# Where the transposes of the quantized activations stand among the self-attention's tiles

## The chip, the core and the metric

The kernel runs on one core of a Trainium2 chip. The core has a matrix engine (TensorE, PE in the profile; its weight loads are PEld), a vector engine (VectorE, DVE), a scalar engine (ScalarE, ACT), GpSimd (POOL) and SyncE (SP), which here only issues DMAs. Each engine works through its own queue in order; semaphores make one wait for another. PE writes into PSUM, eight banks of 128 partitions by 512 floats; DVE and ACT read PSUM, POOL does not. The metric is the device time in microseconds of one execution, here the median of three runs.

## The reference

The layer takes `x` (16 x 64 x 1024, so 1024 rows) and a context (16 x 1024 x 1024) and computes, in float32:

```
x = x + cross_attention(layernorm(x), ctx)         # 32 heads, 8 key/value heads, 32 wide
x = x + self_attention(layernorm(x))               # the same heads, rotary positions, 64 keys each
x = x + ffn(layernorm(x))

ffn(x):
    beta = mean(|x|) per row
    xq   = clip(round(x * sqrt7 / (beta + eps)), -8, 7) * beta      # 4-bit activations
    gate = xq @ ternary(w_gate).T * scale;  up = xq @ ternary(w_up).T * scale    # 1024 -> 2752
    inter = up * relu(gate)^2
    out  = int8(inter) @ ternary(w_down).T * scale                  # 2752 -> 1024
```

`ternary(w)` rounds `w / mean|w|` to -1, 0 or 1. The values of `xq` without their scale are small integers, so the feed-forward matmuls are done on bf16 activations against fp8 weights.

## The kernel before

The 1024 rows are eight tiles of 128 (two batches each). The kernel first does the cross-attention for all batches (up to about 1305 us), then the output projection and the second layer norm, and then, from about 1486 us, the part that the change touches. All order is written by hand: the program's text is the order on every engine.

**The loop over tiles (lines 1250 to 1304).** Iteration `t` (0 to 8) works on two tiles of the self-attention at once: `two` is tile t, whose scores are made, and `last` is tile t-1, which is finished. Its parts, in order:
- `transpose3(t - 2)`: eight PE transposes (L941) of the 4-bit activations of tile t-2 from `xq3` into one PSUM bank, and one ACT copy (L942) from there into `xqT[t - 2]`, the left operand of the gate/up matmuls.
- `two.by_key()`: 32 small matmuls (L781) into `w`, which fills four PSUM banks, and two ACT copies (L791) to SBUF.
- `last.subtract()` (DVE L830): the scores less their maxima, which come back by DMA.
- `last.exponentials()` (ACT L833), `last.values()` (PE L841 and L852 into the same `w`, then ACT copies L860 and L863), `last.finish()` (PE transposes L873 and L876, DVE L878 and L883, then the residual sum on POOL, L889).
- `two.maxima(0)`, `two.maxima(1)` (DVE L800, L801) and `two.row()` (DVE L813, L817; then SP sends the maxima to DRAM, L821, and fetches them back spread over partitions, L825).
- `quantize(t - 1)` in four pieces on DVE with a little POOL: `statistics` (L187 and after; needs L889), `magnitude` (L179, L921), `scaled` (L924 to L927), `rounded` (L930, L932; writes the single `xq3` buffer that the transposes read).

**Fillers.** Between these parts `fill()` takes the next piece of other PE work from a list. Up to t=3 these are pieces of the second half's key, value and query projection (24 pieces; a query chunk is two pieces and ends in `rotary`: ACT L719, DVE L720 and L721, POOL L722 and L723). From t=4 on they are 32 gate/up steps `(n, tt)`: column chunk n of 344 columns for row tile tt of 0 to 3. A step is 8 gate matmuls and 8 up matmuls (L959), a Relu on ACT (L967), a multiply on DVE (L968) and one on POOL (L971). After the last row tile of a chunk, `fetch(n + 3)` issues two DMAs on SP (L949) for weights of a later chunk. The iterations t=0 to 3 hold six fillers, t=4 nine (two ahead of `by_key`), t=5 to 7 seven, t=8 what is left. Only four pieces are left for t=3.

**PSUM banks.** `w` has four banks. The other four are m0, m1, t0 and t1. `four_tile` goes round them (m1, t0, t1, m0), and the even gate/up steps take t1 for the gate product and m0 for up, the odd steps m1 and t0. `transpose3` takes t0 or t1 through `t_tile`, which flips a bit at every allocation of a t bank, whoever makes it. A bank can be written again when its last reader is done: Relu for a gate product, DVE's multiply for an up product.

**The last loop (lines 1308 to 1334).** 32 more steps, chunks 0 to 7 for row tiles 4 to 7; the first nine are for tiles 4 to 6 and the tenth is the first on tile 7. Steps 0 and 1 use two banks (`m_tile`), from step 2 on the four banks of `w` are used. Beside given steps stand the quantization and the transposes of tile 7, the DMAs of the down weights (`fetch_down`), and from step 9 on the 8-bit quantization and down projection. After step 9 PE works on almost without a gap.

Of the kernel before, what the change touches and what calls it, by code (L numbers as in the profile page):

```python
# [25 lines left out]
NT = B * NQ // P  # L26
# [23 lines left out]
def kernel(  # L50
# [33 lines left out]
    def t_tile(shape, dtype, name, n=None):  # L84

        turns["t"] ^= 1
        n = turns["t"] if n is None else n
        return ps_t.tile(shape, dtype, tag=f"t{n}", name=name)

    def m_tile(name):  # L90
        turns["m"] ^= 1
        return ps_m.tile([P, 512], F32, tag=f"m{turns['m']}", name=name)

    def four_tile(name):

        turns["four"] = (turns["four"] + 1) % 4
        if turns["four"] < 2:
            return ps_m.tile([P, 512], F32, tag=f"m{turns['four']}", name=name)
        return t_tile([P, 512], F32, name, turns["four"] - 2)
# [10 lines left out]
    def place(kb, shape, dtype=F32):  # L110

        first, n = round(kb * 256), math.prod(shape) * mybir.dt.size(dtype)
        a = arena[:, first : first + (n + 3) // 4]
        if dtype != F32:
            a = a.bitcast(dtype)
        a = a[:, : math.prod(shape)]
        if len(shape) > 1:
            names = [f"a{i}" for i in range(len(shape))]
            sizes = dict(zip(names[1:], shape[1:]))
            a = a.rearrange(f"p ({' '.join(names)}) -> p {' '.join(names)}", **sizes)  # L120
        return a
# [790 lines left out]
    def quantize(t):  # L912

        xn = place(xn3_at, [DIM])
        statistics, normalize = layernorm(xn, xs[t], f"n3_{t}")
        b = beta[:, t : t + 1]
        rb = small.tile([P, 1], F32, tag="rb", name=f"rb_{t}")

        def magnitude():
            normalize()  # L920
            nc.vector.tensor_reduce(b, xn, AX.X, ALU.add, apply_absolute_value=True)  # L921

        def scaled():
            nc.vector.tensor_scalar_mul(b, b, 1.0 / DIM)  # L924
            nc.vector.tensor_scalar_add(rb, b, EPS)
            nc.vector.reciprocal(rb, rb)
            nc.vector.tensor_scalar(xn, xn, SQRT7, rb, ALU.mult, ALU.mult)  # L927

        def rounded():
            nc.vector.tensor_scalar(xn, xn, -8.0, 7.0, ALU.max, ALU.min)  # L930
            xq3[t] = place(xq_at, [DIM], BF)
            nc.vector.tensor_scalar(xq3[t], xn, MAGIC, MAGIC, ALU.add, ALU.subtract)  # L932
            nc.gpsimd.tensor_tensor(cgate[:, t : t + 1], b, wscale[:, 0:1], ALU.mult)
            nc.gpsimd.tensor_tensor(cup[:, t : t + 1], b, wscale[:, 1:2], ALU.mult)

        return [statistics, magnitude, scaled, rounded]

    def transpose3(t):
        tp = t_tile([P, KC, P], BF, f"xqp_{t}")
        for k in range(KC):  # L940
            nc.tensor.transpose(tp[:, k, :], xq3[t][:, bass.ts(k, P)], ident_b)  # L941
        nc.scalar.copy(xqT[t], tp)  # L942

    def fetch(n):

        wbs[n] = []
        for i in range(2):
            q = wb_ring.next([KC, CW], F8)
            nc.sync.dma_start(q.rearrange("p k o -> p (k o)"), ternary[i][n % NCH])  # L949
            wbs[n].append(q)  # L950

    def gate_up(n, t, banks):

        c = n % NCH
        relu, prod = relu_ring.next([CW]), prod_ring.next([CW])
        for i in range(2):
            ps = banks(i)
            for k in range(KC):
                nc.tensor.matmul(  # L959
                    ps[:, :CW],  # L960
                    lhsT=xqT[t][:, k, :],
                    rhs=wbs[n][i][:, k, :],
                    start=(k == 0),
                    stop=(k == KC - 1),
                )
            if i == 0:
                nc.scalar.activation(relu, ps[:, :CW], AF.Relu, scale=cgate[:, t : t + 1])  # L967
        nc.vector.scalar_tensor_tensor(  # L968
            prod, ps[:, :CW], cup[:, t : t + 1], relu, ALU.mult, ALU.mult
        )  # L970
        nc.gpsimd.tensor_tensor(inter[t][:, bass.ts(c, CW)], prod, relu, ALU.mult)  # L971
# [26 lines left out]
    def fetch_down():  # L998
        wd_rows = ternary_d.rearrange("c p f -> (c p f)").rearrange("(i h) -> i h", h=DIM)
        nc.gpsimd.memset(wds[NIC - 1][LAST:], 0.0)  # L1000
        for c0, c1 in ((0, 16), (16, NIC - 1)):
            nc.sync.dma_start(
                place(112 if c0 == 0 else 22, [c1 - c0, DIM], F8),
                wd_rows[c0 * P : c1 * P].rearrange("(c p) h -> p c h", p=P),
            )
        nc.sync.dma_start(wds[NIC - 1][:LAST], wd_rows[(NIC - 1) * P :])
# [43 lines left out]
    def fill(n=1):  # L1050
        for _ in range(n):
            if fillers:
                fillers.pop(0)()

    with tc.manual_schedule():
# [36 lines left out]
        tiles = [(kT, v)]  # L1092
        for n in range(2 * B):

            b = n // 2
            if n % 2 == 0:
# [8 lines left out]
                elif b + 1 < B:  # L1105
                    kT, v, steps = project_fast(b + 1)
# [14 lines left out]
            for i in range(4):  # L1121
# [25 lines left out]
                t = n // 4 - 1  # L1147
# [101 lines left out]
        two, last = None, None  # L1249
        for t in range(NT + 1):  # L1250
            two, last = (Tile2(t, w) if t < NT else None), two
            late = t >= NT // 2
            if t == NT // 2 - 2:
                for n in range(2):
                    fetch(n)
            if t == NT // 2:
                fill(len(fillers))
                fetch(2)
                steps = [(n, tt) for n in range(NCH) for tt in range(NT // 2)]

                steps[:12] = [s for s in steps[:12] if s[1] < 3] + [(n, 3) for n in range(3)]

                def beside(n, tt):
                    gate_up(n, tt, lambda i: four_tile(f"gu_{n}_{tt}_{i}"))
                    if tt == NT // 2 - 1:
                        fetch(n + 3)

                fillers += [lambda s=s: beside(*s) for s in steps]
            if t > 1:
                transpose3(t - 2)  # L1270
            if t == NT // 2:
                fill(2)
            pieces = quantize(t - 1) if last and two else []

            def piece():
                if pieces:
                    pieces.pop(0)()

            if two:
                two.by_key()  # L1280
            if last:
                last.subtract()
            fill()
            if last:
                last.exponentials()
            if two:
                two.maxima(0)
            fill()
            if last:
                last.values()  # L1290
            if two:
                two.maxima(1)
            fill()
            if last:
                last.finish()
            if two:
                two.row()
            for n in range(4):
                if n == 3 and not late and two:
                    break  # L1300
                fill()
                piece()
            while pieces:
                piece()
# [1 line left out]


        pieces = quantize(NT - 1)
        pieces[0]()
        pieces[2:] = [lambda two=pieces[2:]: [piece() for piece in two]]  # L1310
        steps = [(n, t) for n in range(NCH, 2 * NCH) for t in range(NT // 2, NT)]

        steps[:12] = [s for s in steps[:12] if s[1] < NT - 1] + [s for s in steps[:12] if s[1] == NT - 1]
        beside = {9 + 2 * i: step for i, step in enumerate(sum(map(quantize8, range(4)), []))}
        beside[0] = lambda: (pieces[1](), fetch_down())
        beside[2] = pieces[2]
        beside[6] = lambda: transpose3(NT - 1)
        for t in range(2):
            for i, step in enumerate(transpose8(t)):
                beside[14 + 8 * t + 2 * i] = step  # L1320
# [2 lines left out]
        for i, (n, t) in enumerate(steps):  # L1323
            if i == 2:
                ps_w_closed.close()
                more = ctx.enter_context(tc.tile_pool(name="ps_g", bufs=4, space=PSUM))
            if more:
                gate_up(n, t, lambda j: more.tile([P, 512], F32, tag="g", name=f"g_{n}_{t}_{j}"))
            else:
                gate_up(n, t, lambda j: m_tile(f"gu_{n}_{t}_{j}"))  # L1330
            if i in beside:
                beside[i]()
            if t == NT - 1 and n + 3 < 2 * NCH:
                fetch(n + 3)
# [80 lines left out]
```

## Time and profile before

| | us |
|---|---|
| three runs, median (lowest to highest) | 1909.86 (1909.07 to 1910.14) |
| the profiled execution's own time | 1907.71 |
| its span, first to last instruction | 1905.9 |
| PE busy | 1833.2 (96%) |
| DVE busy | 1240.4 (65%) |
| ACT busy | 898.7 (47%) |
| POOL busy | 883.2 (46%) |

Within the loop over tiles, one iteration from a `transpose3` to the next (start of L941):

| iteration | length | PE busy | DVE busy | mean granted clock |
|---|---|---|---|---|
| t=2 | 34.72 | 28.32 | 21.92 | 0.89 |
| t=3 | 31.40 | 21.16 | 19.16 | 0.83 |
| t=4 | 32.45 | 28.14 | 22.47 | 0.92 |
| t=5 | 28.44 | 24.15 | 21.24 | 0.86 |
| t=6 | 27.88 | 23.61 | 21.18 | 0.92 |
| t=7 | 27.40 | 23.11 | 21.39 | 0.94 |

Times are from the span's start. A row of the timeline gives start and duration, the engine, the line of the program, the tile written and read, and in brackets how long the engine stood idle before it and what ended that. A row of waits gives who waited for whom, the total, the number of times and the longest. The granted clock is a share of PE's full clock: 0.50 is half speed. Busy time of PE includes time at half clock, so the span, not the busy share, tells what a stage costs.

### The profile page before, as it was taken

The numbers are of one execution on the slowest core, as the hardware profiler recorded it, in microseconds if no ns is written. First come the engines' busy times: TensorE is split into PE (matmuls) and PEld (weight loads), VectorE is DVE, ScalarE is ACT, GpSimd is POOL, SyncE is SP. The second block draws the span as 40 slices with busy tenths as digits, with TensorE's granted clock in tenths as the row PEclk, the third lists the DMA queues.
The fourth block names the chain that finished last, engine by engine and source line by source line (L and its number), as shares of the span: only waits on it lengthen the run. The fifth ranks groups of instructions, "written<-read, shape, count | busy, mean of one in ns | idle before, by whom it ended". The sixth has DMA issues, their size and how long they took to land.

```text
span 1905.9 us, 26357 instructions
## 1 busy us (share of the span) xinstructions
PE 1833.2 (96%) x10880; PEld 1085.9 (57%) x10880; DVE 1240.4 (65%) x1468; ACT 898.7 (47%) x924; POOL 883.2 (46%) x479
## 2 busy tenths in 40 slices
PE   8999999999899999999999999999999977898999
PEld 5445556566566666666566566564454533555654
DVE  3012678788778878878878788777332465775564
ACT  1243566566567667667667676443001223242221
POOL 1000457647555656656656657547014243434420
PEclk9999999999999999999999999999999998999999
DMA  8234478778677877777777786560020121423201
GB/s 338 74 111 158 178 232 252 222 233 259 166 232 244 236 227 246 223 249 236 226 255 231 222 256 188 155 254 34 4 89 0 24 75 38 105 56 117 78 27 52
DMA packets 65927, 314.64 MB, mean 165 GB/s; under 512 B 10192, under 2 KB 19344, under 8 KB 49040
## 3 DMA queue, kind: packets, MB, share of 16 engines
q1 hardware_dynamic: 56592, 252.15, 37.5%
q0 software_dynamic: 8064, 58.72, 15.6%
q10 hardware_dynamic: 1152, 2.10, 0.3%
q8 instruction: 85, 1.39, 0.3%
q14 instruction: 34, 0.28, 0.0%
HBM read 293.74 MB, written 19.20 MB: 164 GB/s over the span
## 4 chain that ended last, share of the span: by engine, by line
PE 69%; DVE 3%; POOL 1%; issue 1%; DMA 1%; ACT 0%; ACTq 0%
PE v L426 16%; PE z L407 10%; PE q L250 6%; PE wo L250 6%; PE t L575 5%; PE o L637 5%; PE d L1033 4%; PE p L407 4%; PE g L959 4%; PE gu L959 2%; PE k L250 1%; PE v L740 1%; PE w L781 1%; POOL arena L889 1%; PE o L647 1%
## 5 line engine op out<-in xcount | busy, mean ns | idle before, releaser
L628 POOL TENSOR_TENSOR arena<-arena 128x1024 f32<-128x1024 f32 x192 | 542.0, 2823 | 20.6 <-ACT arena L619 8.5
L426 PE MATMUL v<-arena 128*128 128x256 f32 x1792 | 405.2, 382 | 1.2 <-ACT arena L442 1.2
L594 DVE TENSOR_TENSOR arena<-t,arena 128x512 f32<-128x512 f32 x384 | 258.7, 687 | 211.3 <-PE t L575 155.6
L426 PEld LDWEIGHTS v<-arena 128*128 128x128 f32 x1792 | 336.8, 190 | 78.3 <-issue 29.2
L618 DVE TENSOR_TENSOR arena<-arena 128x2048 f32<-128x2048 f32 x128 | 373.6, 2958 | 4.4 <-DMA arena<-tops 4.4
L587 ACT COPY arena<-t 128x1024 f32<-128x1024 f32 x256 | 254.7, 1009 | 208.5 <-PE t L575 118.9
L619 ACT ACTIVATE arena<-arena 128x2048 f32<-128x2048 f32 x128 | 244.6, 1911 | 168.8 <-DVE arena L618 168.1
L625 POOL TENSOR_TENSOR arena<-arena 128x1024 f32<-128x1024 f32 x32 | 77.1, 2410 | 521.6 <-ACT arena L619 498.0
L407 PE MATMUL z<-arena 128*128 128x512 f32 x560 | 259.9, 606 | 11.8 <-DMA arena<-in_ctxT 8.9
L250 PE MATMUL q<-arena 128*128 128x512 f32 x512 | 226.3, 599 | 0.6 <-ACT arena L287 0.6
L407 PEld LDWEIGHTS z<-arena 128*128 128x128 f32 x560 | 103.1, 191 | 138.4 <-issue 118.7
L250 PEld LDWEIGHTS q<-arena 128*128 128x128 f32 x512 | 96.5, 192 | 119.6 <-issue 117.1
L575 PE MATMUL t<-arena 32*128 32x256 f32 x2048 | 146.6, 400 | 1.2 <-ACT arena L346 1.2
L959 PEld LDWEIGHTS <-arena 128*128 128x128 bf16 x1024 | 100.5, 99 | 60.5 <-issue 6.8
L591 DVE TENSOR_REDUCE arena<-t 128x512 f32<-128x1024 f32 x64 | 74.7, 1204 | 88.9 <-PE t L575 88.9
L575 PEld LDWEIGHTS t<-arena 32*128 32x128 f32 x2048 | 93.1, 184 | 66.6 <-issue 61.4
L971 POOL TENSOR_TENSOR arena<-arena 128x344 f32<-128x344 f32 x64 | 72.3, 1130 | 119.3 <-DVE arena L968 109.4
L637 PE MATMUL o<-arena 128*32 128x256 f32 x2048 | 123.8, 382 | 0.0
L250 PE MATMUL wo<-arena 128*128 128x512 f32 x256 | 112.3, 595 | 0.3 <-ACT arena L287 0.3
L407 PE MATMUL p<-arena 128*128 128x512 f32 x224 | 108.2, 605 | 0.0
L637 PEld LDWEIGHTS o<-arena 128*32 128x32 f32 x2048 | 60.0, 109 | 68.7 <-issue 32.0
L722 POOL TENSOR_TENSOR arena<-arena 128x512 f32<-128x512 f32 x20 | 35.5, 1774 | 136.0 <-DVE arena L720 136.0
(142 smaller groups left out, 1980.4 us busy)
## 6 DMA issues: line engine op xcount, KB each, us to landing
arena<-in_ctxT SPq DMA_DIRECT2D x31, 2048.0 KB, 11.8
arena<-in_ctxT POOLq DMA_DIRECT2D x56, 1024.0 KB, 11.3
arena<-in_ctxT SPq DMA_DIRECT2D x28, 1024.0 KB, 12.0
arena<-tops SPq DMA_DIRECT2D x48, 512.0 KB, 4.7
arena<-in_wg SPq DMA_DIRECT2D x32, 688.0 KB, 4.6
arena<-in_wu SPq DMA_DIRECT2D x32, 688.0 KB, 6.3
arena<-in_wd SPq DMA_DIRECT2D x32, 688.0 KB, 8.8
arena<-ternary SPq DMA_DIRECT2D x32, 344.0 KB, 3.7
```

The lines of the kernel that those rows point to most:

```text
L250: nc.tensor.matmul(made[0], lhsT=lhsT(k), rhs=rhs(k), start=(k == 0), stop=(k == KC - 1))
L407: nc.tensor.matmul(held[n], lhsT=weights[:, k, :], rhs=what()[:, k, :], start=(first and k == 0), stop=(k == 3), skip_group_check=not first,)
L426: nc.tensor.matmul(held[n][:, bass.ts(at, KVD)], lhsT=ctx_halves[b, h][:, k, bass.ts(kts[at], P)], rhs=wkvs[:, k, KVD:], start=(k == 0), s ...
L575: nc.tensor.matmul(ws[jj // 2][:, jj % 2, a, :], lhsT=self.kT[rows, self.g, bass.ts(i * 2 + a, P)], rhs=two_tiles[self.b // 2 % 2][rows, s ...
L587: nc.scalar.copy(pt[:, 2 * mine : 2 * mine + 2], ws[mine])
L594: nc.vector.tensor_tensor(m, w[:, :, a], m, ALU.max)
L618: nc.vector.tensor_tensor(pt, pt, by.to_broadcast([P, 4, 2, 256]), ALU.subtract)
L619: nc.scalar.activation(pt, pt, AF.Exp)
L625: nc.gpsimd.tensor_tensor(acc, pt[:, :, 0], pt[:, :, 1], ALU.add)
L628: nc.gpsimd.tensor_tensor(acc, acc, pt[:, :, a], ALU.add)
L637: nc.tensor.matmul(self.po[bass.ts(jj, HD), 0:256], lhsT=self.v[:, kt, bass.ts(self.g * 4 + jj, HD)], rhs=self.pts[i][:, jj, a, :], start= ...
L959: nc.tensor.matmul(ps[:, :CW], lhsT=xqT[t][:, k, :], rhs=wbs[n][i][:, k, :], start=(k == 0), stop=(k == KC - 1),)
```

## The change

Five edits in the loop over tiles and the last loop:
- `transpose3(t - 2)` no longer opens the iteration. It stands after the second filler, ahead of `last.values()`; at t=5 it stands one filler earlier, ahead of `last.exponentials()`.
- The first twelve gate/up steps run over tiles 0 and 1 first, then tile 2, then tile 3 (before: tiles 0 to 2 per chunk, then tile 3).
- At t=4 the last filler is left out, as it is at t=0 to 3, so one step more remains for t=8, where it comes after `values`.
- In the last loop the four quantization pieces of tile 7 stand beside steps 1, 2, 4 and 5 (before: the first ahead of the loop, then beside 0 and two beside 2) and its transposes beside step 8 (before: 6).
- Steps 0 and 1 of the last loop use the four banks m0, m1, t0 and t1.

```diff
-                steps[:12] = [s for s in steps[:12] if s[1] < 3] + [(n, 3) for n in range(3)]
+                steps[:12] = [
+                    (n, tt) for tiles in ((0, 1), (2,), (3,)) for n in range(3) for tt in tiles
+                ]
...
-            if t > 1:
-                transpose3(t - 2)
             if t == NT // 2:
                 fill(2)
...
             if last:
                 last.subtract()
             fill()
+            if t == NT // 2 + 1:
+                transpose3(t - 2)
             if last:
                 last.exponentials()
             if two:
                 two.maxima(0)
             fill()
+            if t > 1 and t != NT // 2 + 1:
+                transpose3(t - 2)
             if last:
                 last.values()
...
             for n in range(4):
-                if n == 3 and not late and two:
+                if n == 3 and two and t <= NT // 2:
                     break
                 fill()
                 piece()
...
         pieces = quantize(NT - 1)
-        pieces[0]()
-        pieces[2:] = [lambda two=pieces[2:]: [piece() for piece in two]]
...
-        beside[0] = lambda: (pieces[1](), fetch_down())
-        beside[2] = pieces[2]
-        beside[6] = lambda: transpose3(NT - 1)
+        beside[0] = fetch_down
+        for i, piece in enumerate(pieces):
+            beside[(1, 2, 4, 5)[i]] = piece
+        beside[8] = lambda: transpose3(NT - 1)
...
-                gate_up(n, t, lambda j: m_tile(f"gu_{n}_{t}_{j}"))
+                gate_up(n, t, lambda j: four_tile(f"gu_{n}_{t}_{j}"))
```

## The prediction

> **What bounds the kernel now.** I read the chain that ended last first: 69% of the span is PE, so time comes out only where PE stands still or runs slowly. The waits of PE between 1533 and 1760 us, where the change lies, are three groups:
>
> ```profile
> PE xqp L941 <- DVE arena L932: 40.2, 7, 10.2
> PE gu L959 <- DVE arena L968: 3.0, 1, 3.0
> PE w L873 <- ACT arena L863: 1.7, 1, 1.7
> ```
>
> The first is the wait ahead of each of the seven `transpose3(t - 2)` for DVE's `rounded` (L932). The timelines of PE, of DVE and of ACT around iteration t=5 (start, duration; the bracket is the idle time before) show what stands behind it:
>
> ```profile
> 1638.88 1.03 PE L941 MATMUL xqp<-ident_b,arena 128*128 128x128 bf16 x8 [4.32 <-DVE arena L932]
> 1639.85 2.01 PE L781 MATMUL w<-arena 32*64 32x256 f32 x32
> 1641.79 6.20 PE L959 MATMUL gu<-arena 128*128 128x344 fp8e4 x32
> 1647.92 1.09 PE L841 MATMUL w<-arena 64*32 64x256 f32 x32
> 1653.48 9.56 PE L959 MATMUL gu<-arena 128*128 128x344 fp8e4 x64
> 1667.32 1.04 PE L941 MATMUL xqp<-ident_b,arena 128*128 128x128 bf16 x8 [4.29 <-DVE arena L932]
> ...
> 1637.54 1.28 DVE L932 TENSOR_SCALAR arena<-arena 128x1024 bf16<-128x1024 f32 x1
> 1638.74 2.28 DVE L830 TENSOR_TENSOR arena<-arena 128x2048 f32<-128x2048 f32 x1
> ...
> 1644.80 1.90 ACT L833 ACTIVATE arena<-arena 128x2048 f32<-128x2048 f32 x1
> ```
>
> PE is free at 1634.6 and waits 4.3 us, then does transposes, `by_key` (L781) and two gate/up steps (L959) before `values` (L841). The subtraction (L830) that `values` needs was done at 1641.0 already. So DVE and PE form a loop: from `values` DVE goes on without a pause to the next `rounded`, and from `rounded` PE needs 9.1 us to the next `values`. The granted clock (columns: stretch, length, PE busy, clock, DMA share, GB/s):
>
> ```profile
> 1663.00:1664.00 1.00, 0.04 (x1) 1.00 1.12 229
> 1664.00:1665.00 1.00, 0.00 (x0) 1.00 0.75 145
> 1665.00:1666.00 1.00, 0.00 (x0) 0.52 0.99 327
> 1671.00:1672.00 1.00, 1.00 (x5) 0.57 0.00 0
> 1738.00:1741.00 3.00, 0.24 (x2) 1.00 0.96 305
> ```
>
> Each of the seven gaps (4.28 to 10.2 us) halves the clock; the gaps of 1.72 and 3.04 us near 1732 and 1740 do not. Interpolating the rows, the clock falls at 1538.74, 1572.88, 1600.18, 1637.74, 1665.04, 1695.76 and 1723.06, all whole multiples of 3.413 us apart, and rises 3.9 to 5.7 us after PE restarts. Work at half clock takes twice its time: 2.6, 2.3, 2.0, 2.8, 2.3, 1.7 and 1.7 us lost, 2.2 in the mean.
>
> **The change part by part.** The sum is made in the profiled execution, 1907.71 us (span 1905.9), 2.15 below the median of the three runs; I take the difference off the median.
>
> *Transposes moved (the main term).* I cut each iteration at the end of `rounded(t-2)` and at the start of `values(t-1)`. Before, the first stretch takes 11.18, 10.89, 13.08, 9.10, 8.55, 8.04 and 6.97 us for t=2 to 8 (L932's end to L841's start), 67.8 together. After, `by_key` and the steps no longer wait for `rounded`; PE runs them while DVE finishes, and what is left from `rounded` is the subtraction (2.28, begun 0.08 before L932 ends) and the exponentials (1.90), with 0.2 of hand-over: 4.3 us. That holds at t=3 and t=7. In the others the transposes themselves come late, since they now stand between the second step and `values` and need a PSUM bank that alternates between t0 and t1 (parities counted from the allocations; before, the seven fall on t0):
> - t=2: bank t0, held by the query chunk just finished, whose copy (L719, 0.69) stands behind the exponentials on ACT; then 8 transposes (0.46 at full clock, as at 1754.2) and hand-overs: 5.5.
> - t=6 and t=8: bank t1, held by the second step's gate product; its Relu (0.45 to the next start) is behind the exponentials: 5.3 each.
> - t=4: the two steps of `fill(2)` now run while DVE still quantizes tile 2, so their two multiplies (L968, 0.49 from start to start) come ahead of the subtraction; bank t0 is freed by the fourth step's multiply, behind subtraction (2.28), multiply, first maxima (2.40) and multiply. 0.98+2.28+0.49+2.40+0.49+0.46+0.2 = 7.3.
> - t=5: transposes stand one step earlier and must wait for `rounded`; then 0.46, hand-over 0.26, ACT's copy (1.01, 0.1), and step (0,3), which reads them, 2.35: 4.3, equal to the exponentials.
>
> Sum 36.3, gain 31.5. The ACT copy (L942, 1.01) that moves in ahead of the copies of `values` is hidden by `values` itself (1.9); uncovered it would cost 1.0 each.
>
> *The stretch `values` to `rounded`* (19.3 us at t=5 to 7) is DVE's and stays, but at t=4 it holds three steps instead of four: one multiply, gain 0.5. Step order: (0,3), (1,3), (2,3) still come in that order and so do their DMAs on SP; the third now stands behind `row`'s DMAs, and weights land 3.7 us after issue against 7.9 to their use (`values`, a step, finish, a step): 0. The step put off from t=4 is done in t=8 after `values`.
>
> *The end.* From `values(7)` to the first step on tile 7 before: 1729.51 to 1759.35, 29.8 us, with waits of 1.72 (copies of `values`) and 3.04 (two banks, a multiply behind the statistics). After: `values` 1.95, a step 2.35 that covers the copies, finish 1.3, nine steps 21.15 on four banks, transposes 0.46, and a new wait of 1.4 for their copy (0.26+1.01+0.1), since the next step reads tile 7: 28.6. Gain 1.2. The quantization pieces are spread beside steps 1, 2, 4 and 5 and DVE has 1.8 us idle per step there: 0.
>
> *Full clock:* 31.5+0.5+1.2 = 33.2 gained.
>
> *The clock.* PE's work per loop is `by_key` 1.05, seven steps 16.45, transposes 0.46, `values` 1.9, finish 1.3: 21.2. With loops of 24.6 (t=6), 23.6 (t=7) and 24.6 (t=8, no `by_key`) it waits 3.5, 2.5 and 4.5. In the same way 3.6 at t=2 and 2.4 at t=3 (four and two query halves of 3.45), 4.3 at t=4 (a step waiting for a multiply), then 2.6 more, and 3.05+1.4 at t=5. The nearest rows: a gap of 3.04 kept the clock, 4.28 halved it. Finer: laid on the raster of 3.413 us, the clock fell at 1665.04 with PE idle for the last 2.00 us of one raster step, and was kept at 1740.13 with PE idle for the last 1.89. So I take it that about 1.95 us idle within one step is what counts. Then 4.3 and 4.5 (t=4, t=8) always halve it, 3.5 and 3.6 in nearly 9 of 10 positions on the raster, 3.05 in 3 of 4, and 2.4 and 2.5 in a little over half: 5.7 drops in the mean. At 2.2 us each, less 0.7 at t=4, where DVE's maxima cover a part, that is 11.8. Unlike before, the slow work after a gap is `values` and finish, which DVE waits for, so nothing else hides it. Bounds: none, 0; all seven at 2.7, 19.
>
> The Trainium skill ("TensorE: Matmul & The Clock Gate", Part 1) says the clock is halved after at least one idle window of about 3.4 us, free-running. The spacing of the drops agrees with a free-running window, but the drop 2.0 us after the last matmul does not agree with a window wholly idle. By that reading few of the new gaps would cost anything and the sum would be 1877.
>
> Net gain 33.2 - 11.8 = 21.4: 1888.5, say **1888** us.
>
> **The rivals.**
> 1. The clock stays up: gaps of 2.4 to 3.6 behave like those of 1.72 and 3.04. For: these two rows. Against: the drop at 1665.04. Gain 33.2: 1877.
> 2. The shift's DMA becomes the last wait. `row` sends maxima out and back (L821, L825) and the subtraction needs them. At t=0 DVE waited for it until 8.6 us after L817; at t=6 it came 10.7 us after and cost 0.34. DVE itself gets there in 10.25, which the change does not lengthen (9.8 at t=4). If it lands after 11.5 us, four loops lose 1.3 each: 1894. For: the margin is thin. Against: six of the eight rows show no wait.
> 3. The wait comes back in full: `values` now waits for ACT or a bank as long as the transposes waited for DVE, and the stretch from `rounded` stays at its old length. Then 0.5+1.2 remain: 1908, no change. Against: the exponentials (1644.80) stood behind ACT's copies of `by_key`, which move ahead by the whole gap, and ACT is busy for 10.0 of 27.9 us in a loop.
> 4. Slower: DVE's stretch, now the bound, swells, as POOL and DVE work more at once. L930 takes 0.69 us in some rows and 1.64 in others, L932 0.69 and 1.28. For: both fell beside POOL instructions. Against: `rounded` meets POOL's L934 already, and the worst values of all its operations add 1.1 per loop, 7.8 in seven: 1896. It decides from 3.1 us per loop (21.4/7); at 4 us the time is 1916.
>
> **How the numbers follow.** Forecast 0.60 (its own range, three drops at 1.7 to seven at 2.7, is 1882 to 1896), rival 1 0.14, rival 2 0.17, rival 3 0.04, rival 4 0.05. The range 1876 to 1900 takes in rival 1, rival 2 up to 13 us of landing, and rival 4 at its worst rows. A change under 0.2% (3.8 us) is about what a measurement here cannot tell from none. Faster 0.91, within 0.04 (rival 3), slower 0.05 (rival 4).
>
> **What would show it.** `by_key` (L781) starting with no idle before it at t=2 to 7; L941 between L959 and L841; PE's wait for L932 gone but at t=5 (3 us); new waits of PE for ACT's L833, L967, L719 and L942; `rounded` to `values` 4.3 to 7.3 us; DVE nearly without idle from L878 to L830; clock drops in five or six of the loops; no wait of 3.04 for L968 after 1700 us. I am wrong if `values` still starts 8 us after `rounded`, if L830 waits for DMA by over 1 us in several loops, or if the stretch from `values` to `rounded` grows beyond 19.3 us.

## The result and the profile after

| | before | after |
|---|---|---|
| median of the runs shown, four each (lowest to highest), us | 1910.00 (1909.07 to 1910.42) | 1883.66 (1879.04 to 1885.47) |
| profiled execution, us (span) | 1907.71 (1905.9) | 1883.49 (1881.7) |
| ratio after to before (95% interval) | | 0.9859 (0.9841 to 0.9877) |

The change saves 26.3 us in the medians and 24.2 in the profiled executions; 1888 was forecast, so the measured median is 4.3 us below it. One of the eleven executions of e4 below took 6146.08 us, over three times the others, and is left out of its ratio; why is not known. The waits of PE in the changed kernel from 1508 to 1745 us:

```profile
PE xqp L941 <- ACT arena L967: 7.2, 2, 4.2
PE w L841 <- ACT arena L833: 4.1, 2, 2.1
PE gu L959 <- DVE arena L968: 3.7, 1, 3.7
PE xqp L941 <- ACT arena L719: 3.0, 1, 3.0
PE xqp L941 <- DVE arena L932: 2.2, 1, 2.2
PE gu L959 <- ACT arena L942: 1.1, 1, 1.1
PE g L959 <- ACT arena L942: 1.1, 1, 1.1
PE xqp L941 <- DVE arena L968: 0.7, 1, 0.7
```

Of the 40.2 us of waiting for `rounded` (L932) 2.2 are left, at t=5. Over all PE waits 23.1 us in this stretch, where it waited 45. Iteration t=6 on PE, DVE and ACT:

```profile
1645.46 1.12 PE L781 MATMUL w<-arena 32*64 32x256 f32 x32
1646.52 4.87 PE L959 MATMUL gu<-arena 128*128 128x344 fp8e4 x32
1654.41 1.01 PE L941 MATMUL xqp<-ident_b,arena 128*128 128x128 bf16 x8 [3.02 <-ACT arena L967]
1655.35 1.96 PE L841 MATMUL w<-arena 64*32 64x256 f32 x32
...
1648.49 1.28 DVE L932 TENSOR_SCALAR arena<-arena 128x1024 bf16<-128x1024 f32 x1
1649.70 2.28 DVE L830 TENSOR_TENSOR arena<-arena 128x2048 f32<-128x2048 f32 x1
...
1652.01 1.91 ACT L833 ACTIVATE arena<-arena 128x2048 f32<-128x2048 f32 x1 [2.95 <-DVE arena L830]
1653.83 0.53 ACT L967 ACTIVATE arena<-gu,cgate 128x344 f32<-128x344 f32 x1
```

`by_key` and two steps now run while DVE still rounds. Then PE waits: the exponentials end at 1653.9, the Relu behind them frees the transposes' bank, the transposes run, and only then `values`. From `rounded`'s end (1649.77) to `values` (1655.35) it is 5.58 us; before it was 8.55. Both stretches of all loops, from the ends of L932 and the starts of L841:

| | t=2 | t=3 | t=4 | t=5 | t=6 | t=7 | t=8 | sum |
|---|---|---|---|---|---|---|---|---|
| `rounded` to `values`, before | 11.18 | 10.89 | 13.08 | 9.10 | 8.55 | 8.04 | 6.97 | 67.8 |
| forecast at full clock | 5.5 | 4.3 | 7.3 | 4.3 | 5.3 | 4.3 | 5.3 | 36.3 |
| after | 5.71 | 4.20 | 8.07 | 6.82 | 5.58 | 4.20 | 5.58 | 40.2 |
| `values` to the next `rounded`, before | 23.54 | 20.51 | 19.37 | 19.34 | 19.34 | 19.35 | | |
| after | 24.62 | 22.16 | 18.42 | 19.35 | 20.42 | 19.34 | | |

The granted clock of the changed kernel around four gaps (stretch, length, PE busy, clock, DMA share, GB/s):

```profile
1575.00:1576.00 1.00, 1.00 (x33) 0.83 0.00 0
1654.00:1655.00 1.00, 0.59 (x6) 0.59 0.00 0
1681.00:1684.00 3.00, 3.00 (x55) 1.00 0.03 5
1701.00:1702.00 1.00, 0.00 (x0) 0.98 0.00 0
```

In the whole loop it falls at t=2, 3, 4, 5, 6 and 8 and stays up at t=7 (third line). At t=2, 3 and 6 `values` and what follows it run at half clock, and those are the lengthened entries of the last row.

### The profile page after: what moved, and what is told of

Read it like the earlier page. It is cut to its first block, busy times and chain, and to the rows that moved or that the text cites. A ratio compares the mean times of both kernels' runs of the same rounds, so it can differ in the third digit from the quotient of the medians.

```text
span 1881.7 us, 26358 instructions
## 1 busy us (share of the span) xinstructions
PE 1829.8 (97%) x10880; PEld 1084.2 (58%) x10880; DVE 1239.9 (66%) x1468; ACT 898.2 (48%) x924; POOL 883.1 (47%) x479
## 4 chain that ended last, share of the span: by engine, by line
PE 67%; DVE 3%; issue 1%; ACT 1%; POOL 1%; DMA 1%; ACTq 0%; DVEq 0%; POOLq 0%
PE v L426 16%; PE z L407 10%; PE wo L250 6%; PE q L250 5%; PE t L575 5%; PE o L637 5%; PE d L1033 4%; PE g L959 4%; PE p L407 4%; PE gu L959 2%; PE k L250 1%; PE v L740 1%; DVE arena L830 1%; PE w L841 1%; PE o L647 1%
## 5 line engine op out<-in xcount | busy, mean ns | idle before, releaser
L959 PEld LDWEIGHTS <-arena 128*128 128x128 bf16 x1024 | 99.7, 99 | 63.3 <-issue 8.5
L971 POOL TENSOR_TENSOR arena<-arena 128x344 f32<-128x344 f32 x64 | 72.8, 1140 | 109.9 <-DVE arena L968 98.7
```

What stands on the lines that cost most here:

```text
L959: nc.tensor.matmul(ps[:, :CW], lhsT=xqT[t][:, k, :], rhs=wbs[n][i][:, k, :], start=(k == 0), stop=(k == KC - 1),)
```

## The experiments

The theory under test: DVE's stretch from `values` to `rounded`, then subtraction, exponentials and `values` form a closed loop, and the change gains by taking the transposes and what stood behind them out of it; what it loses again is half clock after the new gaps and PSUM banks that come free late. The rivals are in the expectations. All ratios are to the kernel before, run beside on the same chip. Stretches, waits and clocks are those of each run's profiled execution.

**The two parts apart.** The kernel before with the last loop's edits alone, and the changed kernel with the old last loop:

```diff
 # e1: before, and only this
-        pieces[0]()
-        pieces[2:] = [lambda two=pieces[2:]: [piece() for piece in two]]
...
+        beside[0] = fetch_down
+        for i, piece in enumerate(pieces):
+            beside[(1, 2, 4, 5)[i]] = piece
+        beside[8] = lambda: transpose3(NT - 1)
...
+                gate_up(n, t, lambda j: four_tile(f"gu_{n}_{t}_{j}"))
 # e2: the changed kernel without these lines
```

> The kernel before with the edits of the last loop alone (quantization of tile 7 beside steps 1, 2, 4 and 5, transposes beside step 8, four banks for steps 0 and 1). Loop theory (the gain comes from the stretch between `rounded` and `values`): PE's wait of 3.04 us for L968 goes, a wait of 1.4 us for the copy of the transposes comes, so 1.6 us faster than before, about 1908.4; the seven waits for L932 stay at 40 us. Rival (the last loop carries the gain): 1890 or less.

> The changed kernel with the last loop as before. Loop theory: the seven stretches from `rounded` to `values` stay at about 40 us in sum (67.8 before), PE waits 3 us for L968 in the last loop and no longer 1.1 us for L942, so 1.6 us slower than the changed kernel, about 1885. Rival (the last loop carries the gain): above 1900.

e1 took 1905.55 us (0.9985, 0.9976 to 0.9994), e2 1884.52 (0.9875, 0.9859 to 0.9892). The last loop's edits are worth 2.9 us by themselves, with an interval from 1.1 to 4.6; the seven waits for L932 are untouched in e1 (40.2 us) and the wait of 3.04 for L968 is gone. The move of the transposes carries the gain, together with the order of the first twelve steps and the filler put off from t=4: e2 holds all three, and no run parts them. In e2's profiled execution, the fastest of its four, with a mean clock of 0.994 against 0.990, the clock was at half ahead of `values` only at t=4 and 8. The seven stretches came to 5.30, 4.20, 7.60, 4.24, 5.17, 4.20 and 5.58, together 36.29: the forecast at full clock was 36.3.

**The bank of the transposes.** The changed kernel with the bank named:

```diff
-        tp = t_tile([P, KC, P], BF, f"xqp_{t}")
+        tp = t_tile([P, KC, P], BF, f"xqp_{t}", n)
...
-                transpose3(t - 2)
+                transpose3(t - 2, (1, 1, 1, 0, 0, 1, 0)[t - 2])
```

> The changed kernel with the PSUM bank of each moved transpose named: t1 at t=2, 3, 4, 7 and t0 at t=5, 6, 8, each a bank whose last reader is done early. Loop theory with banks as a part of it: the stretches at t=2, 6 and 8 fall from 5.6 to 4.3 us and at t=4 from 8.1 to about 6; PE's waits for L719 and L967 give way to shorter ones for L833; gaps shorten from 3.0 to 2, so fewer clock drops. 5 to 8 us faster than the changed kernel, 1876 to 1879. Rival (the bank doesn't matter since the exponentials end last anyway): within 1 us of the changed kernel.

1876.76 us (0.9834, 0.9821 to 0.9848), below the changed kernel by 6.9 in the medians and 4.8 by the ratios (0.9834 against 0.9859), about as expected (5 to 8). The stretches at t=2, 6 and 8 are 4.19, 4.20 and 4.20. PE at t=6:

```profile
1647.71 0.61 PE L941 MATMUL xqp<-ident_b,arena 128*128 128x128 bf16 x8 [1.13 <-DVE arena L968]
1649.17 1.10 PE L841 MATMUL w<-arena 64*32 64x256 f32 x32 [0.85 <-ACT arena L833]
```

One wait of 3.02 us has become two of 1.13 and 0.85 with the transposes between them, at full clock. t=4 missed: 7.28 instead of about 6.

**The price of half clock.** The kernel before, with matmuls that nothing reads in PE's gap at t=5 to 8; its outputs are unaffected:

```diff
             if t > 1:
+                if t > NT // 2:
+                    extra = t_tile([P, 512], F32, f"extra_{t}", 0)   # e9: (0, 1, 0, 1)[t - 5]
+                    n = (2, 4, 5, 7)[t - 5]
+                    for i in range(24):
+                        nc.tensor.matmul(extra[:, :CW], lhsT=xqT[0][:, i % KC, :],
+                                         rhs=wbs[n][0][:, i % KC, :], start=True, stop=True)
                 transpose3(t - 2)
```

> The kernel before with 24 further gate matmuls (products that nothing reads) in PE's gap ahead of the transposes at t=5 to 8; they take 3.5 of the gap's 4.3 us. Nothing else moves. Clock part of the theory: the clock stays at full speed in these four loops, the steps after the gap take 4.9 us instead of 5.5 to 6.5, and 2.8+2.3+1.7+1.7 = 8.5 us go: about 1901.5. Rival (the work at half clock runs beside DVE and costs nothing): 1910. Rival (the whole gain of the change is the clock): the same four loops would take 23 to 24 us each as in the changed kernel, some 1894.

1905.40 us (0.9981, 0.9972 to 0.9990): 3.6 us less than before, not 8.5. The trace says why: at t=6 and 8 the bank was still held by a multiply, so the extra work ran until 1.9 and 3.4 us after `rounded` (the transposes start at 1665.70 and 1720.67, `rounded` ends at 1663.82 and 1717.25) and delayed what it should have quickened. At t=5 and 7 it fitted, and the stretches fell to 6.58 and 6.46. So I repeated it with the other bank there:

> As the first run with further gate matmuls in the gap of the kernel before, but at t=6 and t=8 they go to bank t1 rather than t0. In the first run they stood there behind a multiply of the last step and ended 1.7 us after `rounded`; at t=5 and t=7 they fitted and the stretch to `values` fell from 9.10 and 8.04 to 6.58 and 6.46 us. Clock part of the theory: all four stretches come to 6.5 us (at t=8 5.3, no `by_key`), so 2.5+2.0+1.6+1.7 = 7.8 us less than before, about 1901. Rival (the work at half clock costs less than that outside the two loops seen): 1904 or more.

1901.82 us (0.9961, 0.9949 to 0.9974). The stretches at t=5 to 8 are 6.59, 6.46, 6.45 and 5.31 us. PE at t=5, and its clock:

```profile
1636.55 3.68 PE L1274 MATMUL extra<-arena 128*128 128x344 fp8e4 x24 [0.34 <-DVE beta L924]
1640.50 0.62 PE L941 MATMUL xqp<-ident_b,arena 128*128 128x128 bf16 x8 [0.27 <-DVE arena L932]
1641.05 1.12 PE L781 MATMUL w<-arena 32*64 32x256 f32 x32
1642.22 4.87 PE L959 MATMUL gu<-arena 128*128 128x344 fp8e4 x32
1647.03 1.09 PE L841 MATMUL w<-arena 64*32 64x256 f32 x32
```

```profile
1639.00:1641.00 2.00, 1.73 (x17) 1.00 0.00 0
1641.00:1645.00 4.00, 3.94 (x54) 1.00 0.15 25
```

Transposes 0.62 instead of 1.03, `by_key` 1.12 instead of 2.01, two steps 4.87 instead of 6.20. Half clock is worth 7.5 us in four loops, and work without use makes the kernel faster by that. The same four stretches come to 32.7 us before, 24.8 here, 22.2 in the changed kernel, whose clock still falls at t=5, 6 and 8, and 19.2 in e2, where it falls only at t=8. So of the 13.5 us between the kernel before and e2, 7.9 go when the clock stays up with the order as it was, and 5.6 more with the new order. In these loops much of what the change gains is slow work that used to stand between `rounded` and `values`. For t=2 to 4, where the larger part of the gain lies, no run parts clock from order.

**The loop itself.** The changed kernel with `rounded` behind the next subtraction; the work on every engine is the same:

```diff
             pieces = quantize(t - 1) if last and two else []
+            before, held = held, None
+            if pieces and t != NT // 2:
+                held = pieces.pop()
...
                 last.subtract()
+            if before:
+                before()
```

> The changed kernel with `rounded` put behind the next iteration's subtraction (not for tile 3, which t=5 needs at once). DVE does the same work; only the order of 2.0 us of rounding and 2.3 us of subtraction is exchanged. Loop theory (subtraction, exponentials, `values`, DVE's stretch is the closed loop that sets the time): the exponentials start up to 2.0 us sooner in t=2, 3, 6, 7, 8; the maxima's DMA lands 8.6 to 10.7 us after L817, so 1 to 1.6 us of it can be had per loop: 5 to 8 us faster than the changed kernel, 1876 to 1879. Rival (the loop is bound by DVE's total work or by PE, so order within DVE doesn't matter): within 2 us of the changed kernel, 1882 to 1886.

1873.05 us (0.9811, 0.9798 to 0.9825): below the changed kernel by 10.6 us in the medians and 9.2 by the ratios, more than the 5 to 8 expected. So the order within DVE's queue matters, which the rival denied. From `values` to `values` the loops into t=2, 3, 4, 7 and 8 are 1.8, 2.4, 1.5, 2.2 and 1.4 us shorter; at t=6 only 0.6. DVE there, in this kernel:

```profile
1644.67 2.29 DVE L830 TENSOR_TENSOR arena<-arena 128x2048 f32<-128x2048 f32 x1 [1.59 <-DMA arena<-tops]
1646.88 0.69 DVE L930 TENSOR_SCALAR arena<-arena 128x1024 f32<-128x1024 f32 x1
1647.60 0.69 DVE L932 TENSOR_SCALAR arena<-arena 128x1024 bf16<-128x1024 f32 x1
```

The subtraction is early enough to wait for the maxima's DMA, which the prediction held to be the next limit. And L932 takes 0.69 us here where it took 1.28, at t=6 to 8 alike, which is a part of the surplus (1.8 us). The mean clock is 0.995, and it fell four times in the loop instead of six. What the order alone is worth is not parted from these two.

**Transposes behind `values`, and both.**

```diff
-            if t > 1 and t != NT // 2 + 1:
-                transpose3(t - 2)
             if last:
                 last.values()
+            if t > 1 and t != NT // 2 + 1:
+                transpose3(t - 2, (0, 1, 0, 0, 1, 0, 1)[t - 2])
```

> The changed kernel with the moved transposes behind `values` instead of ahead of it (t=5 as it is), each in a bank that the next step doesn't use. Loop theory: the stretch from `rounded` to `values` is 4.2 us at t=2, 3, 6, 7, 8 and about 5.5 at t=4, where only the two multiplies of `fill(2)` remain ahead of the subtraction; 33 to 34 in sum at full clock, some 2 us less than with free banks alone, so about 1875. Rival (where the transposes stand is of no matter once their banks are free): as with the free banks, 1877.

> Both edits: transposes behind `values`, `rounded` behind the subtraction. Loop theory: the gains add, as `rounded` is no longer between the subtraction and `values` in any way: 5 to 8 us below the kernel with the transposes behind `values`, about 1868 to 1870, if the DMA of the maxima doesn't end last. If it does (second rival of the prediction), DVE's subtraction shows waits for DMA of 0.5 to 2 us in most loops and the gain is under 3 us: 1872 to 1875.

e6 took 1881.59 us (0.9851, 0.9838 to 0.9864), e7 1872.05 (0.9808, 0.9795 to 0.9822). e6 missed by 6.6 us. Its stretches to `values` are as short as with free banks (34.5 in sum against 34.7), but four of the six stretches behind `values` are longer, 3.7 us in sum: 25.61, 22.57, 18.87, 19.85, 21.43 and 19.79 us from t=2 on against 23.57, 22.16, 18.42, 19.91, 19.36 and 20.98 in e3. Its five waits of `values` for the exponentials are 14.1 us in all, up to 3.7, with no transposes to break them, and the clock fell more (mean 0.990 against 0.992). In e3 the transposes ahead of `values`, in a free bank, split the gap. In e7 waits for the DMA came to 4.0 us and the gain beyond e5 is 1.0, within the intervals: the gains don't add, as the DMA rival had it.

**A third step ahead of `values`.** e7, with one `fill()` more ahead of `last.values()` at t=6 and 7, one less at the end of these iterations, and the banks of their transposes named anew:

> As the run with both edits, and at t=6 and 7 a third gate/up step ahead of `values` (one fewer at the end of the iteration). It takes 2.35 us of PE's wait for the exponentials of about 2.4. Loop theory: PE's work doesn't bound the loop, so the loops stay as long, but PE's idle time is spread and the clock drops fall away in two loops: 0 to 4 us below the run with both edits, 1865 to 1870. Rival (PE is the bound in these loops): the third step delays `values` by what it exceeds the wait, 1 to 2 us slower per loop, 1870 to 1874.

1873.95 us (0.9815, 0.9801 to 0.9828), not to be told from e7. `values` came 1.8 us after `rounded` at t=6 and 7 instead of 0.67, so the third step was the last to end there by 1.1 us, and DMA waits rose to 5.9 us. The mean clock was 0.995 in both: the drop of e7 at 1646.05 (t=6) is gone in e8, and one at 1692.71 (t=8) has come, where `values` now waits 4.76 us instead of 2.75.

**Both, with free banks ahead of `values`** (e3's and e5's edits):

> Transposes ahead of `values` in named free banks, and `rounded` behind the subtraction. Loop theory: the transposes wait for `rounded` only, which ends as the exponentials do, so `values` comes as soon as with the transposes behind it: 1870 to 1874, like that run (1872). If banks and order were two separate gains of 7 and 11 us that add: 1866.

1868.27 us (0.9782, 0.9769 to 0.9795), between the two expectations, and the fastest kernel here: 15.4 us below the changed one in the medians, 14.7 by the ratios. What parts it from e7 stays open: the profiled executions of the two differ by only 0.6 us in span (1869.4 and 1870.0), the medians by 3.8. That profiled execution of e10 is the slowest of its four and has the lowest clock (0.993, the others 0.995 to 0.997), so the trace shows little of what made the others faster. Its waits for the DMA, 4.1 us, are no shorter than e7's 4.0.

**No wait at t=5.** e7, with seven steps at t=4 and four at t=8, so that t=5 runs like the others (the transposes behind `values` there too, their banks named anew):

```diff
-                fill(2)
+                fill(1)
...
-            if pieces and t != NT // 2:
+            if pieces:
...
-            if t == NT // 2 + 1:
-                transpose3(t - 2)
```

> The kernel with transposes behind `values` and `rounded` behind the subtraction, and t=4 with seven gate/up steps (one ahead of `by_key` rather than two), so that t=5 no longer needs tile 3's transposes ahead of `values`; t=8 has four steps. Loop theory: the stretch at t=5 falls from 5.9 us to about 0.7 while the stretch ahead of it grows by 2.0 (`rounded` behind the subtraction), one multiply less at t=4 (0.5), one step more at t=8 (2.35, where PE has nothing to wait for): 1.4 us faster, about 1870.5. Rival (the DMA of the maxima ends last there as at t=6 to 8): no gain, 1872 to 1874.

1872.63 us (0.9804, 0.9791 to 0.9818): no gain. The stretch at t=5 did fall, from 5.9 to 0.67 us, but the one behind it went from 22.97 to 28.32: PE waited 3.38 for the exponentials, ran `values` at half clock (1.96 instead of 1.09), and then 2.11 for the copy of the transposes that the next step needs. The waits for the DMA (0.72 and 1.33 at the two subtractions around it) are the smaller part.

## Why the prediction was right

- **What bounds the kernel.** Right. The loop of DVE's stretch and the way from `rounded` to `values` was the reading that carried the forecast; e5 bears it out, by an exchange of places in DVE's queue that gained 9 to 11 us with what came along. DVE's part is not quite without a pause, as the prediction had it: behind `values` of t=5 in the kernel before it waits 0.79 and 0.66 us for PE (L959 and L876) and 0.41 and 0.16 for POOL.
- **Transposes moved, 31.5 us at full clock.** Right: 36.3 us forecast for the seven stretches, 36.29 in e2, where the clock fell ahead of `values` only at t=4 and 8. That the sums agree to a hundredth is luck: single stretches are off by up to 0.3 us, both ways. The bank terms were right too (t=2, 6 and 8 at 5.2 to 5.6 in e2, and 4.2 with a free bank in e3).
- **`values` to `rounded`.** 0.5 us of gain forecast at t=4, 0.95 measured (19.37 to 18.42): besides the multiply, L932 took 0.69 us there instead of 1.28.
- **The end, 1.2 us gained.** Right at full clock: in e7, where the clock stays up there, it takes 28.85 us from `values(7)` to the first step on tile 7 (1694.60 to 1723.45), with 0.46 of the moved transposes in it, so 28.4 for the 28.6 forecast. In the changed kernel it didn't come: from `values(7)` to the first step on tile 7 it is 30.24 us after (1704.89 to 1735.13) against 29.84. The waits of 1.72 and 3.04 are gone and the new one is 1.10 (forecast 1.4), but `values` and what follows ran at half clock and took that back. e1 measures these edits at 2.9 us with an interval from 1.1.
- **The clock, 11.8 us.** The mis-sized term, by 2.4 us. Drops: 5.7 in the mean forecast, six seen. Their cost: 3.9 us in the stretches to `values` (40.2 less 36.3), 1.1, 1.7 and 1.1 in the stretches behind (24.62 against 23.54, 22.16 against 20.51, 20.42 against 19.34), and 1.6 at the end (30.24 against the 28.6 forecast): 9.4. The first and the last of these are read against the forecast's own values at full clock, which e2 (36.29) and e7 (28.4) bear out. So the full-clock gain was 24.2+9.4 = 33.6 for 33.2 forecast, and nearly the whole miss in the profiled execution (1883.5 for 1886.3) is the 2.4 us by which the drops cost less. The rest of the miss in the medians comes from the executions profiled: the forecast kept the 2.15 us by which that of the kernel before lies below its median, and that of the changed kernel lies only 0.2 below its own. Half clock lasted only 3.2 to 3.4 us of work at t=2, 3 and 6 (1.6 to 1.7 us lost each, where 2.2 was taken), and at t=4, where PE worked 5.3 us at half clock, the stretch grew by 0.8, so 1.9 were covered by DVE and not 0.7.
- **The finer rule** (about 1.95 us idle in one step of a 3.413 us raster) held in the changed kernel, and roughly elsewhere. The drops interpolate to 1544.94, 1575.66, 1596.14, 1623.46, 1654.18 and 1701.96, whole multiples of 3.413 apart to within 0.02. At t=3 PE was idle from 1572.95 to 1574.95, 2.00 us within one raster step, and the clock fell. At t=7 it was idle from 1677.83 to 1679.97, longer, but the raster's boundary at 1678.07 leaves 1.90 in one step, and the clock stayed. Over the raster steps of all thirteen traces between 1500 and 1760 us that begin at full clock, it never fell with less than 1.84 us idle in the step and always with more than 2.03; of the sixteen steps in between, eight show a drop and eight don't. So the rule is a band, not a line.
- **Rival 1, no drops,** and with it the strict reading of the Trainium skill's rule ("TensorE: Matmul & The Clock Gate", Part 1: an idle window of about 3.4 us): six drops, one after a gap of 2.00 us. The free-running window agrees with the trace, a wholly idle one does not.
- **Rival 2, the DMA of the maxima:** not in the change (L830 waits only in the first loop, 1.10), but in e5, e7, e8, e10 and e11 it is there with 2.8 to 5.9 us in all, the first loop's 0.8 to 1.2 included. It is one of the limits behind this one.
- **Rivals 3 and 4** did not come: PE's waiting halved, and DVE's stretch grew only where PE was at half clock. One reading in rival 4 was wrong: it is not POOL's L934 that `rounded` meets (last section).

## What to carry to other kernels

Where an in-order engine waits at the head of an iteration, look for the closed loop through the other engines: measure it from the last result of one to the first use by the other, and move out of it whatever the loop doesn't need. Then look at what is last in the shortened loop (here a PSUM bank, the order of two instructions on DVE, a DMA), since each can be worth something more: here about 5 to 7 us for the bank and 9 to 11 for the order on DVE, while no run took the DMA's wait away. A gap on PE also has a price behind it: two short ones can cost less than one long one (t=6 in e3: 1.13 and 0.85 us at full clock, where one of 3.02 was followed by work at half clock), and even useless matmuls in it can pay, if their bank is free (e9 against e4).

## What the runs showed of the hardware that was not expected

- A gap of 2.14 us kept the clock and one of 2.00 us halved it in the same execution; they lie differently on the 3.413 us raster (1.90 and 2.00 us idle within one step, both in the band above). Executions of one kernel differ too: of the changed kernel's four, the one of 1879.04 us had a mean clock of 0.994, the three of 1883.5 to 1885.5 had 0.990. That the raster's position is the cause of this is argued, not shown, as only one of them has a trace.
- L932 takes 1.28 to 1.30 us beside POOL's multiply of a gate/up step (L971) and 0.69 to 0.71 otherwise, in all 104 executions of the line in the thirteen traces. The kernel before shows how they meet: L971 runs from 1636.99 to 1638.28 on POOL, L932 from 1637.54 to 1638.82 on DVE. POOL's L934 is not the cause: there it starts at 1638.83, behind L932, and where the two do overlap (1539.54 in the kernel before) L932 takes 0.71. So the place of `rounded` alone, without any change of its own, brought it from 1.28 to 0.69 us at t=4 of the changed kernel and at t=6 of e5.
